# A four-layer graph network kernel: first rows in pairs of blocks, degree sums shared between VectorE and GpSimd, norms by ScalarE, and a new place for a block's own pair

## The chip, the cores and the metric

The kernel runs on one core of one Trainium2 chip. A core has five engines that run side by side, each with its own in-order queue: TensorE (PE, matrix products; its weight loads are listed as PEld), VectorE (DVE), ScalarE (ACT), GpSimd (POOL), and SyncE (SP), which here only starts DMA transfers. Matrix products go into PSUM, a small memory of banks; everything else lies in SBUF, which has 128 partitions. The metric is the device time of one execution in microseconds (us); lower is better. A measurement of this kernel can tell a change of about 2% from none.

## The reference

Four graph layers are applied to `x` (4096 rows of 64) with one dense matrix `adj` (4096 x 4096, float32, mostly zero). Each layer normalises the rows, applies a relu and adds its result to `x`:

```
h = relu(layernorm(x)); x = x + L0(h): relu((adj @ h) @ W.T + b)
h = relu(layernorm(x)); x = x + L1(h): q, k, h' = three "lorentz" linears of h
      att = adj * sigmoid((2 + 2 qm @ k.T) / att_scale + att_bias)
      s = att @ h';  s / sqrt(|inner(s)|)
h = relu(layernorm(x)); x = x + L2(h): w = adj / adj.sum(axis=1)          # the degree sums
      agg_i = sum_j w_ij logmap(h_i, h_j); v = agg @ weight + bias
      tanh(|v|) * v / |v|                                                 # the norms
h = relu(layernorm(x)); x = x + L3(h): rank-weighted sum over the last 100 neighbours
```

Layer 2 needs the degree of each row, that is the sum of its row of `adj`. Layers 0 and 1 read the same matrix, so the sums are collected while those layers run. Layer 2's distance between rows i and j is the same both ways, so a pair of blocks (i, j) is worked out once and used for both.

## The kernel before

**Tiles.** `adj` is read from HBM in transfers of 512 KB, each a *group*: two chunks of 128 source rows by 512 target rows, one SBUF tile of 128 x 1024 floats. The 4096 target rows make eight *blocks* (`ib`) of 512, and each block has 16 groups (`g`). The transposed matrix is read, so a group is the moving operand of a product and the sum builds up in a PSUM accumulator `acc`, one per block.

**Layers 0 and 1.** `l0_sums` multiplies each group of `adj` with the normalised rows `HA`. `before0` makes those rows, block by block: a sum over each row, the centred rows, ScalarE's squares, a second sum, a power by GpSimd (`power`, tile `ln_r`), and the product that writes `HA`. After each block, `after0` and `before1` turn its sums into the rows and the q and k of layer 1, with three more powers by GpSimd (`ln_r`, `lo_s` twice). Layer 1 makes, per group, the attention products (`l1_atts`, tile `mm`), ScalarE's sigmoid (`sig`), VectorE's product with `adj`, and the sum on TensorE. The last 12 groups of layer 0 are loaded in alternation with the first 12 of layer 1. Ten SBUF tiles hold groups of `adj` in these layers; a tile is loaded again when all of its readers are done.

**Degree sums.** `degree_sums` adds groups of `adj` into a tile `dg`, one full add of 128 x 1024 on VectorE for each group. The names in `LEFT` say which groups of a block wait until layer 1: four of 16 in blocks 1 to 6. A fold of `dg` and four products with a column of ones (`ones_f`) then give the degrees, in `after0` and, for blocks 1 to 6, again in `after1`.

**Layer 2.** `work` lists the items: for block i the columns J = i, i+1, ..., 7, each in two halves. An item with J > i is a *two*: its tile is also transposed and used for the other direction, through two banks of PSUM (`tr`), and the sums gather in `others`. The two items of the block's own pair (J = i) are shorter: the first (here marked `first`) is whole but its transposes are half as many, the second (`cut`) has half the targets. Per item there are, in order: products on TensorE (`mm`), a square on ScalarE, a clamp on GpSimd (`v<-v`), a logarithm and two exponentials on ScalarE, a VectorE step (`t<-mm,t`), a logarithm, a VectorE step (`t<-t,v`), the weights (`w<-t,adj`, `w<-tr,adj`), and the sums. Functions named `l2_...` hold these steps, and `in_steps` sets their order across neighbouring items. At the end of a block, `after2` turns the sums into rows, through both banks, with a power of eight columns by GpSimd (`r_nn`) for the two roots of the norm; `before3` follows with one more power (`ln_r`).

**Layer 3** is a stage of bf16 products behind layer 2, with masks from `adj` on VectorE.

**Order.** Every engine runs its instructions in the order in which the program issues them. That order is found when the kernel is built: `in_turn` takes, from all the generators (`feed`, `l0_sums`, `degree_sums`, `constants`, the `l2_...` stages and the row chains held in `tail`), the step that can start first by the planner's own costs (`Pace`). The chip then keeps that order even where an instruction waits. Two row chains can be under way at once, and each has one set of small tiles.

Of the kernel before, what the change touches and what calls it, by code (L numbers as in the profile page):

```python
# [18 lines left out]
P = 128  # L19
# [8 lines left out]
LEFT = (3, 7, 11, 15)  # L28
# [30 lines left out]
class Pace:  # L59
# [16 lines left out]
    def cost(self, engine, op, out, ins, rest, kw):  # L76
        n = per_partition(out)
        if engine == "PE":

            w, x = ins[0], ins[1]  # L80
            shape = [32 if k <= 32 else 64 if k <= 64 else 128 for k in (w.shape[0], per_partition(w))]
            change = 0.0 if shape == self.shape else 0.11
            self.shape = shape
            if op == "transpose":
                return change + 0.14
            share = 1 if n < 128 else min(128 * 128 // math.prod(shape), 4)
            passes = 4 if x.dtype == F32 else 1
            return change + max(passes * n / 2400 + 0.06, 0.27 if passes == 4 else 0.06) / share
        if engine == "ACT":
            if any(arg is AF.Sigmoid for arg in rest):  # L90
                n += n // 6
            return 0.18 + n / 1200 + (0.19 if "accum_out" in kw else 0.0)
        if engine == "POOL":
            return 1.65 if ALU.pow in kw.values() or n <= 8 else 0.25 + n / 300
        many = [ap for ap in ins if per_partition(ap) > 1]
        big = max([n] + [per_partition(ap) for ap in ins])
        psum = any(self.name(ap).split("_")[0] in ("mm", "acc", "tr") for ap in ins)
        return 0.12 + big / (1920 if len(many) <= 1 and not psum and op != "tensor_reduce" else 960)
# [38 lines left out]
def kernel(ctx: ExitStack, tc: tile.TileContext, a: dict, out: bass.AP):  # L137
# [93 lines left out]
    halves["both"] = const.tile([P, 2 * CB, 1], F32, name="halves")  # L231
    POOL.memset(halves["both"][:, 0:CB, :], 0.5)
    POOL.memset(halves["both"][:, CB :, :], -0.5)
# [15 lines left out]
    def later_constants():  # L249


        ACT.activation(es, scal[:, 0:3], AF.Exp)

        DVE.reciprocal(att_a, scal[:, 4:5])
        DVE.tensor_scalar(att_a, att_a, 2.0, None, ALU.mult)
        DVE.tensor_add(att_b, att_a, scal[:, 3:4])
        for t, one in [(t, 1.0) for t in rbs] + [(t, 0.25) for t in lbs]:
            POOL.memset(t, 0.0)
            for k in (1, 3):
                POOL.memset(t[:, :, k, 1:2], one)  # L260


        near_f = st["rows"].tile([P, P], F32, name="near_f", bufs=1)
        make_lower_triangular(nc, near_f, val=-STEP, diag=False)
        for q in range(4):
            b = slice(q * Q, (q + 1) * Q)
            DVE.tensor_copy(far[b, :], near_f[b, b])
        diag_f = st["rows"].tile([P, P], F32, name="diag_f", bufs=1)
        DVE.tensor_scalar(diag_f, ident, STEP * MAX_NEIGH, None, ALU.mult)
        DVE.tensor_add(near_f, near_f, diag_f)  # L270
        DVE.tensor_copy(near, near_f)


        DVE.memset(pick, 0.0)
        DVE.memset(spread, 0.0)
        for k in range(KH):
            DVE.memset(pick[:, k, k : k + 1], 1.0)
        for r in range(4):
            b = slice(r * Q, (r + 1) * Q)
            for h in range(2):  # L280
                to = spread[b, h, :, h * NC // 2 : (h + 1) * NC // 2]
                DVE.tensor_copy(
                    to.rearrange("p q (k r) -> p q k r", r=4)[:, :, :, r],
                    ident[b, r * Q : r * Q + KH].unsqueeze(1).to_broadcast([Q, 4, KH]),
                )
# [136 lines left out]
    def before0(ib, st):  # L422
        yield from layernorm_relu(ib, st["h0"][:, cs(ib), :])
# [124 lines left out]
    def after0(ib, acc, st):  # L548
        e = rows.tile([P, W], F32, tag="e", name="e")
        ACT.copy(e, acc)  # L550
        st["acc_free"][ib % 2] = pace.latest
        yield ON_V, lambda: st["dg_done"].get((0, ib))
        dg = st["dg"][0, ib]
        DVE.tensor_add(dg[:, 0, :], dg[:, 0, :], dg[:, 1, :])
        yield TURN

        ps = bank()
        v, n = ps[:, 0 : CB * D].rearrange("p (c k) -> p c k", k=D), CB * D
        for c in range(CB):
            b = slice(c * P, (c + 1) * P)  # L560
            PE.matmul(v[:, c, :], e[:, b], W0T, start=True, stop=True)
            PE.matmul(ps[:, n + c : n + c + 1], dg[:, 0, b], ones_f, start=True, stop=True)
        st["dg_free"][ib % 2] = pace.latest
        yield ON_V
        DVE.tensor_copy(deg[:, cs(ib), :], ps[:, n : n + CB].unsqueeze(2))
        s = rt("h", [P, CB, D])
        DVE.tensor_add(s, v, b0.to_broadcast([P, CB, D]))
        DVE.scalar_tensor_tensor(
            x[:, cs(ib), :], s, 0.0, x[:, cs(ib), :], ALU.max, ALU.add
        )  # L570
        yield ON_V

    def after1(ib, acc, st):
# [3 lines left out]
        yield ON_V, lambda: st["dg_done"].get((1, ib)) if (1, ib) in st["dg"] else 0.0  # L577
        dg = st["dg"].get((1, ib))
        if dg is not None:
            DVE.tensor_add(dg[:, 0, :], dg[:, 0, :], dg[:, 1, :])  # L580
        yield TURN
        ps = bank()
        v, n = ps[:, 0 : CB * D].rearrange("p (c k) -> p c k", k=D), CB * D
        for c in range(CB):
            b = slice(c * P, (c + 1) * P)
            PE.matmul(v[:, c, :], e[:, b], twice, start=True, stop=True)
            if dg is not None:
                PE.matmul(ps[:, n + c : n + c + 1], dg[:, 0, b], ones_f, start=True, stop=True)
        if dg is not None:
            st["dg_free"][ib % 2] = pace.latest  # L590
# [5 lines left out]
        if dg is not None:  # L596
            new = rt("r_c", [P, CB, 1])
            ACT.copy(new, ps[:, n : n + CB].unsqueeze(2))
        yield ON_V
        if dg is not None:  # L600
            DVE.tensor_add(deg[:, cs(ib), :], deg[:, cs(ib), :], new)
# [13 lines left out]
    def after2(ib, acc, others, st):  # L615
# [35 lines left out]
        n = rt("r_nn", [P, 2 * CB, 1])  # L651
        DVE.tensor_reduce(n[:, 0:CB, :], hz, AX.X, ALU.add)
        DVE.tensor_scalar(n[:, 0:CB, :], n[:, 0:CB, :], MIN_NORM * MIN_NORM, None, ALU.max)
        DVE.tensor_copy(n[:, CB :, :], n[:, 0:CB, :])

        POOL.tensor_tensor(n, n, halves["both"], ALU.pow)
        yield ON_S

        th = rt("r_c", [P, CB, 1])
        ACT.activation(th, n[:, 0:CB, :], AF.Exp, scale=-2.0)  # L660
# [3 lines left out]
        DVE.tensor_scalar(th, th, 2.0, -1.0, ALU.mult, ALU.add)  # L664
        DVE.tensor_mul(th, th, n[:, CB :, :])
        DVE.tensor_mul(tr, tr, th.to_broadcast([P, CB, D]))
# [47 lines left out]
    def in_turn(threads):  # L714
# [34 lines left out]
        "dg": {}, "dg_done": {}, "acc_free": [0.0, 0.0], "dg_free": [0.0, 0.0],  # L749
# [70 lines left out]
    def group(layer, ib, g):  # L820
        degree = (g in LEFT and 0 < ib < NB - 1) == (layer == 1)
        return {"layer": layer, "ib": ib, "g": g, "degree": degree, "left": 1 + degree, "at": 0.0}
# [31 lines left out]
    def degree_sums(layer, work):  # L854

        dg = st["dg"]
        for d in work:
            if not d["degree"]:
                continue
            first = (layer, d["ib"]) not in dg  # L860
            yield "DVE", lambda: latest(
                arrival(d, 3.0), st["dg_free"][d["ib"] % 2] if first else 0.0
            )
            if first:
                t = w01.tile([P, G, W], F32, tag="dg", name="dg", bufs=2)
                dg[layer, d["ib"]] = t
                st["dg_free"][d["ib"] % 2] = None
                DVE.tensor_copy(t, d["adj"])
            else:
                t = dg[layer, d["ib"]]  # L870
                DVE.tensor_add(t, t, d["adj"])
            used(d)
            if d is [e for e in work if e["degree"] and e["ib"] == d["ib"]][-1]:
                st["dg_done"][layer, d["ib"]] = pace.latest

    for ib in range(NB):
        follow(with_mark(0, ib, before0(ib, st)))
        tail[-1]["at"] = 4.5 + 0.4 * ib
# [13 lines left out]
    def constants():  # L892
# [5 lines left out]
        later_constants()  # L898
        loads.pop(0)

# [34 lines left out]
    def l1_sums():  # L935
        for pair in pairs:
# [23 lines left out]

    work = [
        {"ib": i, "J": j, "half": s, "g": j * (CB // G) + s, "first": i == j and s == 0,
         "last": j == NB - 1 and s == CB // G - 1, "two": i < j, "cut": i == j and s == 1,
         "left": 1 + (i == j and s == 1), "at": 0.0}
        for i in range(NB) for j in range(i, NB) for s in range(CB // G)
    ]
    twos = [d for d in work if d["two"]]
# [16 lines left out]
    def second_part():  # L984

        yield "ANY", lambda: latest(l1[-1].get("summed"), *st["dg_free"])
# [118 lines left out]
    def l2_turns():  # L1105
        for d in work:
# [6 lines left out]
            if d["first"]:  # L1113
# [24 lines left out]
    def l2_weights2():  # L1138
        k = -1
        for n, d in enumerate(work):  # L1140
            if d["first"]:
# [262 lines left out]
    def l3_sum():  # L1404
# [22 lines left out]
        if d["last"]:  # L1427
# [16 lines left out]
            (l2_coshs(), 0, once), (l2_weights2(), 1, lambda d: 2 if d["two"] else 1 if d["first"] else 0),  # L1444
        ),
        l2_clamps(), l2_gathers(), l3_weights(), l3_pass(), l3_counts(), l3_masks(),
        degree_sums(0, l0), degree_sums(1, l1), constants(),
# [46 lines left out]
```

## Time and profile before

Three runs took 1185.45, 1186.83 and 1261.08 us; the median is 1186.83.

| | |
|---|---|
| profiled execution, its own time | 1186.61 us |
| its span in the trace | 1184.6 us |
| PE / DVE / ACT / POOL busy | 1078.5 / 929.3 / 783.1 / 324.3 us |
| mean granted TensorE clock | 0.976 |
| read from HBM | 269.68 MB, mean 229 GB/s |
| DVE: degree adds of 128x1024 (`dg<-dg,adj`) | 114, 139.2 us |
| PE: products with the column of ones | 112 records, 18.8 us |
| POOL: clamps of 128x1024 | 64, mean 2925 ns |
| POOL: `r_nn` powers of 128x8 | 8, mean 2256 ns |

The span has four stages, which can be told by the tiles that the products read: layer 0 (`acc<-adj,HA`) from 16.7 to 211 us, layer 1 (`acc<-sig,HL`) from 194 to 485 us, layer 2 (`acc<-w,HA`) from 494 to 956 us, and layer 3 (`acc<-wt,S`) from 961 us on. A busy engine need not be the one that bounds its stage, and the means over the span mix stages with different bounds.

How to read the lines below: a row of the windows gives a stretch in us, its length, then the busy time of PE, PEld, DVE, ACT and POOL (with the number of instructions), the granted TensorE clock, the mean busy share of the DMA engines and GB/s. A row of the timeline gives start, length, engine, line of code, operation, tiles (out<-in), shapes, the count of merged instructions, and in brackets the idle time ahead of it with what ended it. Nearly all instructions are issued through one helper, so they share line 129 and are told apart by their tiles.

### The profile page before, as it was taken

The numbers are of one execution on the slowest core, as the hardware profiler recorded it, in microseconds if no ns is written. First come the engines' busy times: TensorE is split into PE (matmuls) and PEld (weight loads), VectorE is DVE, ScalarE is ACT, GpSimd is POOL, SyncE is SP. The second block draws the span as 40 slices with busy tenths as digits, with TensorE's granted clock in tenths as the row PEclk, the third lists the DMA queues.
The fourth block names the chain that finished last, engine by engine and source line by source line (L and its number), as shares of the span: only waits on it lengthen the run. The fifth ranks groups of instructions, "written<-read, shape, count | busy, mean of one in ns | idle before, by whom it ended". The sixth has DMA issues, their size and how long they took to land.

```text
span 1184.6 us, 15638 instructions
## 1 busy us (share of the span) xinstructions
PE 1078.5 (91%) x5367; PEld 449.7 (38%) x5392; DVE 929.3 (78%) x1523; ACT 783.1 (66%) x1250; POOL 324.3 (27%) x172
## 2 busy tenths in 40 slices
PE   3899999999999999889989989999889789999997
PEld 1234444333333333244444444444344333333332
DVE  6888888869988988688888888898989985555550
ACT  1055456777767766789988778787876655555554
POOL 2222321102000010344454464464654420000000
PEclk9898999999999999899999999999998999999999
DMA  7899999865777765535434534444364389888830
GB/s 275 330 405 350 401 378 348 303 216 199 245 249 235 249 232 192 195 107 196 162 128 172 175 121 166 160 150 163 113 206 151 124 343 367 321 314 312 303 112 9
DMA packets 77191, 271.76 MB, mean 229 GB/s; under 512 B 10040, under 2 KB 11064, under 8 KB 77112
## 3 DMA queue, kind: packets, MB, share of 16 engines
q1 hardware_dynamic: 75456, 270.57, 63.7%
q8 instruction: 42, 0.69, 0.2%
q10 hardware_dynamic: 1656, 0.20, 0.1%
q14 instruction: 37, 0.30, 0.1%
HBM read 269.68 MB, written 1.05 MB: 229 GB/s over the span
## 4 chain that ended last, share of the span: by engine, by line
PE 49%; DVE 18%; ACT 11%; issue 10%; POOL 8%; DMA 3%; SPq 0%; ACTq 0%; POOLq 0%; DVEq 0%
PE acc L129 23%; PE mm L129 17%; PE tr L129 8%; DVE dg L129 5%; POOL v L129 4%; ACT wt L129 3%; DVE w L129 3%; ACT v L129 2%; DMA adj<-in_adjT_dram 2%; ACT t L129 2%; DVE t L129 2%; POOL lo_s L129 1%; DVE sig L129 1%; ACT sig L129 1%; POOL ln_r L129 1%
## 5 line engine op out<-in xcount | busy, mean ns | idle before, releaser
L129 PE MATMUL acc<-w,HA 128*65 128x256 f32 (+1 forms) x736 | 256.3, 485 | 13.0 <-DVE others L129 7.1
L129 POOL TENSOR_SCALAR v<-v 128x1024 f32<-128x1024 f32 x72 | 204.8, 2845 | 211.5 <-ACT v L129 205.4
L129 ACT ACTIVATE wt<-mm 128x1024 uint16<-128x1024 f32 x124 | 120.3, 1021 | 94.1 <-PE mm L129 94.1
L129 ACT ACTIVATE sig<-mm,att_b,att_a 128x1024 f32<-128x1024 f32 x128 | 148.3, 1202 | 40.9 <-PE mm L129 39.9
L129 DVE TENSOR_TENSOR sig<-sig,adj 128x1024 f32<-128x1024 f32 x128 | 152.5, 1221 | 25.2 <-ACT sig L129 25.0
L129 PE MATMUL acc<-adj,HA 128*64 128x512 f32 x512 | 128.4, 639 | 24.3 <-DVE HA L129 24.1
L129 DVE TENSOR_TENSOR dg<-dg,adj 128x1024 f32<-128x1024 f32 x114 | 139.2, 1221 | 2.2 <-DMA adj<-in_adjT_dram 0.6
L129 PEld LDWEIGHTS acc<-w,HA 128*65 128x65 f32 x736 | 98.1, 143 | 104.7 <-issue 56.6
L129 PE MATMUL mm<-qT,kT 64*128 64x512 f32 x512 | 129.5, 619 | 3.3 <-ACT sig L129 3.3
L129 PE MATMUL acc<-sig,HL 128*64 128x512 f32 x512 | 123.3, 604 | 1.6 <-DVE sig L129 1.5
L129 DVE SCALAR_TENSOR_TENSOR t<-mm,t 128x1024 f32<-128x1024 f32 x72 | 83.6, 1161 | 44.4 <-ACT t L129 43.9
L129 PE MATMUL acc<-wt,S 128*64 128x512 bf16 (+1 forms) x479 | 97.7, 387 | 3.5 <-issue 2.4
L129 PE MATMUL mm<-RT,LT 64*128 64x512 f32 (+1 forms) x288 | 79.7, 631 | 15.9 <-DVE t L129 15.2
L129 ACT ACTIVATE t<-t 128x1024 f32<-128x1024 f32 x72 | 72.6, 1008 | 31.9 <-DVE t L129 31.3
L129 ACT ACTIVATE v<-mm 128x1024 f32<-128x1024 f32 x72 | 69.8, 970 | 30.7 <-PE mm L129 30.6
L129 POOL TENSOR_TENSOR ln_r<-ln_v,minus_half 128x4 f32<-128x4 f32 x32 | 49.3, 1542 | 148.7 <-DVE ln_v L129 148.7
L129 DVE TENSOR_TENSOR w<-t,adj 128x1024 f32<-128x1024 f32 x72 | 84.0, 1167 | 1.5
L129 DVE SCALAR_TENSOR_TENSOR t<-t,v 128x1024 f32<-128x1024 f32 x72 | 83.7, 1163 | 1.8 <-ACT t L129 0.9
L129 ACT ACTIVATE v<-v,minus 128x1024 f32<-128x1024 f32 x72 | 78.4, 1089 | 7.8 <-POOL v L129 7.7
L129 DVE TENSOR_TENSOR w<-tr,adj 128x512 f32<-128x512 f32 x120 | 77.5, 681 | 1.1 <-PE tr L129 1.1
L129 PE MATMUL tr<-ident,t 128*128 128x128 f32 x480 | 66.1, 280 | 11.9 <-DVE t L129 8.2
L129 DVE TENSOR_SCALAR RT<-adj 128x1024 bf16<-128x1024 f32 x74 | 50.4, 698 | 33.3 <-PE mm L129 33.0
(208 smaller groups left out, 1395.6 us busy)
## 6 DMA issues: line engine op xcount, KB each, us to landing
adj<-in_adjT_dram SPq DMA_DIRECT2D x512, 512.0 KB, 4.8
x<-in_x_dram SPq DMA_DIRECT2D x4, 256.0 KB, 3.7
out_dram<-h SPq DMA_DIRECT2D x8, 128.0 KB, 2.8
b<-in_b_dram ACTq DMA_DIRECT2D x2, 32.0 KB
W<-in_W_dram ACTq DMA_DIRECT2D x3, 16.0 KB, 4.4
W0T<-in_W0T_dram ACTq DMA_DIRECT2D x2, 16.0 KB, 3.4
W1T<-in_W1T_dram ACTq DMA_DIRECT2D x1, 16.0 KB, 3.4
W1T<-in_b_dram ACTq DMA_DIRECT2D x1, 0.2 KB
```

The costliest lines, as they stand in the source:

```text
L129: done = self.tc.keep_in_program_order(getattr(self.engine, op)(*args, **kw))
```

## The change

1. **First rows.** `before0` works on two blocks at a time: four chains of 128 x 512 elements in place of eight of 128 x 256. Their scratch space lies in tiles that layer 1 uses later (`HL`, `qT`) and in `lo_g`, `lo_t`, `lo_n`. The constants of layers 2 and 3, which were made at 36 us of the planner's time, are handed out as late steps (60 and 150 us).
2. **Degree sums.** Of a block's 16 groups VectorE adds eight, in layer 0 (`dg`); GpSimd adds four in layer 0 and four in layer 1, each as two adds of 128 x 512 straight into the block's part of `RT` (a tile that layer 2 fills later; the first group of a block needs one add). VectorE folds `dg` into `RT` with two adds. The products with the column of ones are gone from `after0`, and stand in `after1` for all eight blocks.
3. **Norms of layer 2's rows.** `after2` has no power by GpSimd any more: ScalarE takes a logarithm, two exponentials for the roots, and the exponential for the tanh. VectorE's part is two instructions shorter.
4. **Order of layer 2.** The columns of block i are now i+1, i, i+2, ..., so the own pair comes third and fourth. The first item of a block (`first`) and the start of an own pair (`own`) are told apart.
5. The planner's costs for GpSimd are changed, and `second_part` does not wait for `dg` any more.

```
-LEFT = (3, 7, 11, 15)
+POOL_0, POOL_1 = (3, 7, 11, 15,), (1, 5, 9, 13,)
+FRONT_0, FRONT_1 = (3, 7, 11, 15,), (1, 5, 9, 13,)
+ITSELF = 1
...
-            return 1.65 if ALU.pow in kw.values() or n <= 8 else 0.25 + n / 300
+            if op == "memset":
+                return 0.11 + n / 1200
+            return 0.5 + 0.25 * n if ALU.pow in rest else 0.25 + n / 390
...
-    def before0(ib, st):
-        yield from layernorm_relu(ib, st["h0"][:, cs(ib), :])
+    def before0(k, st):
+        c = slice(2 * k * CB, 2 * (k + 1) * CB)
+        xs, xc, to = x[:, c, :], st["HL"][:, c, :], st["h0"][:, c, :]
+        sq = st["qT"][:, 2 * k * W : (2 * k + 1) * W].rearrange("p (c d) -> p c d", d=D)
+        m, v, r = (rt(name, [P, 2 * CB, 1]) for name in ("lo_g", "lo_t", "lo_n"))
+        DVE.tensor_reduce(m, xs, AX.X, ALU.add)
+        DVE.scalar_tensor_tensor(xc, m.to_broadcast(xs.shape), -1.0 / D, xs, ALU.mult, ALU.add)
+        yield ON_S
+        ACT.activation(sq, xc, AF.Square)
+        yield ON_V
+        DVE.tensor_reduce(v, sq, AX.X, ALU.add)
+        DVE.tensor_scalar(v, v, 1.0 / D, LN_EPS, ALU.mult, ALU.add)
+        power(r, v, -0.5)
+        yield ON_V
+        DVE.scalar_tensor_tensor(to, xc, 0.0, r.to_broadcast(xs.shape), ALU.max, ALU.mult)
+        rows_at[0, 2 * k] = rows_at[0, 2 * k + 1] = pace.latest
...
-        n = rt("r_nn", [P, 2 * CB, 1])
-        DVE.tensor_reduce(n[:, 0:CB, :], hz, AX.X, ALU.add)
-        DVE.tensor_scalar(n[:, 0:CB, :], n[:, 0:CB, :], MIN_NORM * MIN_NORM, None, ALU.max)
-        DVE.tensor_copy(n[:, CB :, :], n[:, 0:CB, :])
-        POOL.tensor_tensor(n, n, halves["both"], ALU.pow)
+        n, one, th = (rt(name, [P, CB, 1]) for name in ("r_n", "r_m", "r_c"))
+        DVE.tensor_reduce(n, hz, AX.X, ALU.add)
+        DVE.tensor_scalar(n, n, MIN_NORM * MIN_NORM, None, ALU.max)
         yield ON_S
-        th = rt("r_c", [P, CB, 1])
-        ACT.activation(th, n[:, 0:CB, :], AF.Exp, scale=-2.0)
+        ACT.activation(n, n, AF.Ln)
+        ACT.activation(th, n, AF.Exp, scale=0.5)
+        ACT.activation(one, n, AF.Exp, scale=-0.5)
+        ACT.activation(th, th, AF.Exp, scale=-2.0)
         yield ON_V
...
     def group(layer, ib, g):
-        degree = (g in LEFT and 0 < ib < NB - 1) == (layer == 1)
+        late = g in (POOL_1 if ib else FRONT_1)
+        by = "POOL" if late or g in (POOL_0 if ib else FRONT_0) else "DVE"
+        degree = by if late == (layer == 1) else None
...
+            yield "DVE", lambda: opened.get(("sums", ib))
+            for c in range(G):
+                DVE.tensor_add(RT[:, ws(ib)], RT[:, ws(ib)], t[:, c, :])
...
+    def degree_sums_beside(work):
         for d in work:
+            if d["degree"] != "POOL":
+                continue
+            to, ib = RT[:, ws(d["ib"])], d["ib"]
+            yield "POOL", lambda: arrival(d, 3.0)
+            if ("sums", ib) in opened:
+                POOL.tensor_tensor(to, to, d["adj"][:, 0, :], ALU.add)
+                yield "POOL", lambda: 0.0
+                POOL.tensor_tensor(to, to, d["adj"][:, 1, :], ALU.add)
             else:
+                POOL.tensor_tensor(to, d["adj"][:, 0, :], d["adj"][:, 1, :], ALU.add)
+                opened["sums", ib] = pace.latest
...
+    def columns_of(i):
+        js = list(range(i + 1, NB))
+        return js[:ITSELF] + [i] + js[ITSELF:]
```

## The prediction

> **What bounds the kernel now.** I read the stages first (windows), then what PE waits for in each (timeline), then the ends of the blocks. The profiled execution took 1186.61 us for a span of 1184.6; the median of the three runs is 1186.83, so the sum below is made against 1186.6.
>
> ```profile
> 15.00:20.00 5.00, 3.30 (x8) 1.01 (x10) 4.85 (x11) 0.42 (x1) 0.42 (x1) 1.00 0.85 322
> 20.00:25.00 5.00, 4.70 (x20) 1.31 (x18) 4.90 (x12) 0.83 (x2) 1.59 (x2) 1.00 0.74 227
> 25.00:30.00 5.00, 3.40 (x16) 0.77 (x12) 3.01 (x8) 0.42 (x1) 1.06 (x2) 1.00 0.48 143
> ...
> 100.00:150.00 50.00, 47.22 (x258) 21.56 (x256) 41.45 (x68) 24.27 (x99) 14.36 (x7) 1.00 0.99 382
> ...
> 300.00:350.00 50.00, 49.62 (x230) 18.37 (x228) 45.00 (x86) 36.09 (x69) 2.85 (x2) 1.00 0.76 251
> ```
>
> Layer 0 (100 to 150) is bound by the loads: DMA busy 0.99, 382 GB/s, with PE close behind. Its start is not: DMA falls to 143 GB/s, because PE has no rows and the ten tiles stay full. Layer 1 (300 to 350) is bound by PE, 49.6 of 50.
>
> ```profile
> 16.22 0.42 DVE L129 SCALAR_TENSOR_TENSOR HA<-ln_xc,ln_r 128x256 f32<-128x256 f32 x1
> ...
> 41.68 0.43 DVE L129 SCALAR_TENSOR_TENSOR HA<-ln_xc,ln_r 128x256 f32<-128x256 f32 x1
> ...
> 42.16 10.18 PE L129 MATMUL acc<-adj,HA 128*64 128x512 f32 x40 [3.42 <-DVE HA L129]
> ```
>
> The first rows come at 16.2 and the last at 42.1 us, with degree adds and constants on VectorE between them. Then the end of a block in layer 2:
>
> ```profile
> 693.35 1.09 PE L129 MATMUL tr<-ident,t 128*128 128x128 f32 x8 [1.29 <-DVE t L129]
> ...
> 698.65 1.13 PE L129 MATMUL mm<-RT,LT 64*128 64x512 f32 x4 [2.11 <-DVE t L129]
> ...
> 700.63 3.46 PE L129 MATMUL acc<-w,HA 128*65 128x256 f32 x8 [0.53 <-DVE w L129]
> ```
>
> ```profile
> 692.10 2.72 POOL L129 TENSOR_TENSOR r_nn<-r_nn,halves 128x8 f32<-128x8 f32 x1 [0.91 <-DVE r_nn L129]
> ```
>
> In steady state PE is full: a two takes 5.85 us, and two of them 12.25 with a wait of 0.5 for `others`. At a block's end PE waits three times (1.29, 2.11, 0.53), and the eight products behind the gap take 3.46 us where they take 1.94 elsewhere, at a granted clock of 0.79 (698 to 702). `e<-acc,others` comes at 679.4, 755.5, 819.3 and 870.9: the gaps 76.1, 63.8 and 51.6 fall by 12.25, so 14.8 us per block remain for its own pair and the rows. PE's own work in that is 8.4 (first item 3.6, cut 2.75, rows 2.0); some 6.4 us per block are lost.
>
> **The change part by part.**
>
> *First rows: -12.* A chain of 512 elements costs VectorE three instructions of 0.69 (rows of 128x512) and one of 0.17, so four chains take 9 us where eight take 15 (1.87 each). ScalarE's square is 0.59 (a 128x512 square), the power of eight columns 2.06 (`lo_s`). From x at 4.4, the first HA ends near 11 and, with the one copy and one add of `dg` between, the last near 20-21. PE then has rows whenever a group is there, and DMA need not fall. Against some 400 GB/s (the windows around reach 409 to 419), 15 to 50 us lack 78+173+257+175+4+85+114 GB/s over 5 us each: 4.4 MB, 11 us. I take 12, as the half clock of 32 to 38 us should go too. Bounds: 4 (only PE's first 6 us, partly) and 16 (first `e` at 45.5 instead of some 30). The constants that go to later steps cost VectorE 4 us in layer 0, beside the loads.
>
> *Products with ones, early attention: -2.* Sixteen records with ones and without (52.3 to 54.2) take 1.9 us, so a block's ones cost 0.95. Eight blocks lose them in layer 0 (7.6 us, mostly behind DMA); layer 1 goes from six to eight, +1.9. In the built order three pairs of attention products (1.92 each) run in layer 0 before its last block, where the old order had them near its end: -5.8 from PE's stage, of which I let a third count, as the row chain of block 7 (33 us, from 212 to 245) holds groups 14 and 15 and would be late next. Bounds -6 and +4.
>
> *Degree sums: +4.* VectorE loses per block of layer 0 11 adds of 1.22 and a copy (14.8 with the fold) and gets 10.6; in layer 1 it loses 5.0. GpSimd gets 120 adds, which no row shows. Nearest:
>
> ```profile
> L129 POOL TENSOR_TENSOR x<-x,b x8: 721/727/1076, 617.8 to 977.2; 128x256 f32<-128x256 f32 x8
> ...
> L129 DVE SCALAR_TENSOR_TENSOR hb<-ln_xc,ln_r x8: 468/1256/1267, 615.1 to 977.6; 128x256 f32<-128x256 f32 x8
> ```
>
> Twice the half-size add is 1.45 us (2.15 by the slowest). Seven in layer 0 and the powers of a chain (1.54+1.74+2.06) fill 15.5 of 21.4 us per block. Three powers per chain can wait behind an add, 1.45 each; behind them wait the chain's VectorE product and its transposes, in a chain of some 45 us with two under way. The second row is the dangerous one: this step takes 0.42 in layer 0 but 1.26 when it starts beside a clamp of GpSimd, +0.84. Both engines then read SBUF. At 0.84 per add, VectorE per layer 1 block has 30 - 5.0 + 8 x 0.84 = 31.7 of 34 us, and in layer 0 17.8 - 14.8 + 10.6 + 7 x 0.84 = 19.5 of 21.4: both fit, with stalls. At 1.45, 36.6 and 23.8: over by 2.6 and 2.4, that is 21 and 17 us in all. So 0 to +38; I take +4, by the 0.84 row.
>
> [...]
>
> *Norms: in the next sum.* Gone are a power of 2.72 us, a copy of 0.17 and one more small VectorE step; ScalarE gets three more of 0.20. The chain is 2.3 us shorter, and the clamp behind the power (0.8 late at 694.8) is not held. What is late next is ScalarE.
>
> *Own pair behind the first pair, with the norms: -18.* The row chain now lies beside the first pair of twos, where PE has 11.7 + 2.0 us of work, and the own pair's light steps come later. ScalarE's load over both pairs is 2 x 5.33 (squares 1.02, logarithms 1.14 and 1.06, exponentials 1.05 and 1.06) + 8.5 (own pair, the cut at half shape) + 3.4 (rows, with the new steps) = 22.5, and 1.2 for the 0.2 us that it waits for VectorE in each item: 23.7. PE needs 20.7. So 23.7 - 12.25 = 11.5 remain per block where 14.8 do now: -3.3 for five blocks and half of that for the sixth. Bounds: PE's 8.4 in six blocks, -38; on the other side the row chain now needs a `tr` bank three times while each two needs both, held for 0.36 to 1.0 us (the ScalarE copies and VectorE reads), +2.5 per block, +15. I take ScalarE's load, as it is the row that binds after the stall. At the start of layer 2 the second-direction tiles are wanted two items sooner; their loads are issued at 485.7, ahead of everything but six groups, and hidden by 490-495's row chain.
>
> *Last block: -2.* It has only its own pair; there the shorter norm counts directly.
>
> Layer 3 stays. Sum: 1186.6 - 12 - 2 + 4 - 18 - 2 = 1156.6, forecast **1157**.
>
> **The rivals.**
>
> *Slower: the shared reads bind VectorE.* Place: layer 1, where every product `sig<-sig,adj` reads SBUF twice. VectorE has 25 us of 34 without adds, so it becomes the bound from 1.1 us of lost time per GpSimd add. At 1.45: +38, and the start's gain is eaten in layer 0: 1186.6 - 20 + 38 = 1205. At 2.15 layer 1 needs 42 us per block and layer 0 28.7: +115, 1280. For it: the 1.26 row; the clamps of layer 2 run mostly beside VectorE steps that read PSUM. Against: 0.84 is under 1.1.
>
> *The first two layers give nothing.* Powers behind adds delay the chains as much as the rows come sooner; layer 2 alone gains: 1186.6 - 20 = 1167.
>
> *The own pair moves without effect.* Banks or ScalarE keep the 14.8; then 1186.6 - 12 - 2 + 4 - 2 = 1175.
>
> *Better.* PE's floor in layer 2 and 15 from the start: 1186.6 - 15 - 2 + 2 - 38 = 1134.
>
> **How the numbers follow.** Forecast (1147 to 1164) 0.52, no gain in the first layers 0.18, own pair without effect 0.12, better 0.08, slower 0.10. A change of 2% is 1163. Faster: 0.48 + 0.08 + 0.04 of the second case = 0.60. Slower by 2% (above 1210.6): 0.08. Same: 0.32. The range takes in half of the better case and both smaller gains, 1138 to 1182; it leaves the slower case out, and what lies under 1138.
>
> **What would show it.** First rows: HA complete by about 21 us, DMA above 350 GB/s from 15 us on, last layer 0 product near 199. Sums: GpSimd's adds near 1.45 us, `sig<-sig,adj` lengthened from its 1.22, PE still 97% busy in layer 1, which ends near 475. Layer 2: 76.1 becomes about 73 between the ends of the blocks, and no PE gap over 1.5 us behind the last sums. Wrong it would be if `sig<-sig,adj` averaged above 1.6 us, if PE waited for `HL` or `qT` in layer 0, or if the new gaps lay behind the cut item.

## The result and the profile after

The changed kernel took **1232.67 us** (median of four runs, 1225.62 to 1235.18), against 1186.14 for the kernel before beside it: a ratio of 1.0388, 95% interval 1.0363 to 1.0413. It is slower by 46 us; the forecast was 1157, and the result lies outside the range, on the side of the slower rival.

The copies that end the blocks' sums (the starts of `e<-acc` and `e<-acc,others`) cut the span into four parts:

| us | layer 0 until its last sum | layer 1 | to layer 2's first sum | from there to the end | span |
|---|---|---|---|---|---|
| before | 211.6 | 274.0 | 105.9 | 593.1 | 1184.6 |
| after | 238.8 | 297.4 | 105.6 | 589.2 | 1231.0 |
| difference | **+27.2** | **+23.4** | -0.3 | -3.9 | +46.4 |

So the whole loss is in the two layers that collect the degree sums, and layers 2 and 3 together gave 4 us of the 20 that were forecast for layer 2. The windows of the kernel after, with the columns of those shown of before:

```profile
15.00:20.00 5.00, 5.00 (x23) 1.52 (x20) 4.45 (x8) 0.63 (x1) 3.91 (x3) 1.00 1.03 409
20.00:25.00 5.00, 4.23 (x20) 0.82 (x16) 4.96 (x3) 0.00 (x0) 4.76 (x4) 1.00 0.66 230
25.00:30.00 5.00, 2.66 (x12) 0.42 (x8) 4.93 (x3) 0.00 (x0) 3.92 (x2) 0.97 0.51 173
...
100.00:150.00 50.00, 44.54 (x202) 18.01 (x204) 42.43 (x50) 23.44 (x89) 29.26 (x19) 0.90 0.86 311
...
300.00:350.00 50.00, 44.31 (x206) 16.62 (x204) 43.70 (x94) 32.49 (x71) 21.47 (x15) 1.00 0.60 199
```

The start is as forecast until 20 us (PE full, 409 GB/s), and then the loads fall again. From 100 to 150 the DMA share is 0.86 where it was 0.99, and in layer 1 PE is busy for 44.3 of 50 us where it was 49.6. VectorE has 42.4 and 43.7 of 50 in these rows: it is not full in either.

What PE waits for in layer 0 (the table of waits; sum in us, number, longest), first before (45 to 212 us), then after (45 to 239 us):

```profile
PE tr L129 <- DVE HL L129: 3.8, 6, 1.2
PE tr L129 <- DVE h L129: 2.5, 2, 1.6
PE tr L129 <- ACT qq L129: 1.1, 2, 0.6
```

```profile
PE tr L134 <- DVE HL L134: 14.6, 7, 4.1
PE tr L134 <- DVE h L134: 7.4, 6, 2.1
PE tr L134 <- ACT qq L134: 5.7, 4, 1.9
```

PE stands at the transposes of the row chains, 28 us instead of 7. In all, PE is idle for 29.1 us between 45 us and the last sum, where it was for 7.7: 21 of the 27 us. The other 6 are longer busy time, at a mean granted clock of 0.94 instead of 0.98. In layer 1 PE's busy time did not grow (267.5 us before, 266.9 after); all 23 us there are idle time.

The VectorE steps that PE waits for have become longer, which the summaries by tile show (shortest, median and longest in ns, first and last start), before and after:

```profile
L129 DVE TENSOR_TENSOR sig<-sig,adj x128: 1217/1220/1227, 187.7 to 481.5; 128x1024 f32<-128x1024 f32 x128
L129 DVE TENSOR_TENSOR HL<-hb,lo_s x8: 412/420/422, 72.4 to 236.9; 128x252 f32<-128x252 f32 x8
```

```profile
L134 DVE TENSOR_TENSOR sig<-sig,adj x128: 1210/1224/2304, 203.6 to 527.6; 128x1024 f32<-128x1024 f32 x128
L134 DVE TENSOR_TENSOR HL<-hb,lo_s x8: 1477/1478/1490, 56.6 to 264.4; 128x252 f32<-128x252 f32 x8
L134 POOL TENSOR_TENSOR RT<-RT,adj x112: 1257/1652/2557, 20.8 to 505.8; 128x512 f32<-128x512 f32 x112
```

More than half of the sigmoid products keep their 1.22 us, the longest take 2.30 (the mean is 1491 ns). GpSimd's own add takes 1.27 when left alone (at 35.38), and up to 2.56: **both** engines lose. And the step `HL<-hb,lo_s` loses 1.06 us all eight times. Why every time in this kernel, the timeline of after shows, one collision in layer 0 (VectorE, GpSimd, PE) and one in layer 1:

```profile
171.11 1.48 DVE L134 TENSOR_TENSOR HL<-hb,lo_s 128x252 f32<-128x252 f32 x1 [1.13 <-POOL lo_s L134]
...
171.04 2.67 POOL L134 TENSOR_TENSOR RT<-RT,adj 128x512 f32<-128x512 f32 x2
...
172.73 0.60 PE L134 MATMUL tr<-ident,HL 128*64 128x128 f32 x4 [1.24 <-DVE HL L134]
...
354.79 3.43 DVE L134 TENSOR_TENSOR sig<-sig,adj 128x1024 f32<-128x1024 f32 x2
...
353.06 4.08 POOL L134 TENSOR_TENSOR RT<-RT,adj 128x512 f32<-128x512 f32 x2 [2.31 <-DMA adj<-in_adjT_dram]
```

`HL` waits for a power by GpSimd. When the power ends, GpSimd goes straight on with the next add in its queue, and VectorE's step starts 0.07 us later beside it. The end of the power thus starts both, here GpSimd's first. In layer 1, two products take 3.43 in place of 2.44 beside two adds that take 4.08 in place of 2.61 (at 64.42, where VectorE is idle).

The boundary of the first two blocks of layer 2 in the timeline of after:

```profile
732.43 0.63 PE L134 MATMUL tr<-ident,t 128*128 128x128 f32 x4 [1.57 <-DVE l L134]
...
751.36 1.93 PE L134 MATMUL acc<-w,HA 128*65 128x512 f32 x4 [1.81 <-DVE w L134]
754.66 1.13 PE L134 MATMUL mm<-RT,LT 64*128 64x512 f32 x4 [1.37 <-DVE t L134]
...
757.01 1.97 PE L134 MATMUL tr<-ident,t 128*128 128x128 f32 x8 [0.89 <-DVE t L134]
758.77 2.58 PE L134 MATMUL acc<-w,HA 128*65 128x512 f32 x4
```

The stall behind the last sums has gone, and the same time stands elsewhere: PE waits for a bank of the row chain at 732, and behind the cut item at 751 to 757, where the products then run longer again (2.58 for 1.88).

### The profile page after: what moved, and what is told of

It reads as the page before. It is cut to its first block, busy times and chain, and to the rows that moved or that the text cites. A ratio compares the mean times of both kernels' runs of the same rounds, so it can differ in the third digit from the quotient of the medians.

```text
span 1231.0 us, 15536 instructions
## 1 busy us (share of the span) xinstructions
PE 1087.4 (88%) x5318; PEld 442.9 (36%) x5344; DVE 950.0 (77%) x1411; ACT 788.9 (64%) x1272; POOL 494.4 (40%) x278
## 4 chain that ended last, share of the span: by engine, by line
PE 39%; DVE 24%; issue 13%; ACT 11%; POOL 8%; DMA 4%; ACTq 0%; POOLq 0%; SPq 0%; DVEq 0%
PE acc L134 19%; PE mm L134 13%; PE tr L134 6%; DVE sig L134 4%; DVE w L134 4%; DMA adj<-in_adjT_dram 3%; ACT wt L134 3%; DVE t L134 3%; POOL RT L134 3%; ACT v L134 2%; DVE dg L134 2%; POOL lo_s L134 2%; ACT t L134 2%; ACT sig L134 2%; DVE r_n L134 1%
## 5 line engine op out<-in xcount | busy, mean ns | idle before, releaser
L134 POOL TENSOR_SCALAR v<-v 128x1024 f32<-128x1024 f32 x72 | 201.0, 2791 | 260.8 <-ACT v L134 230.6
L134 POOL TENSOR_TENSOR RT<-RT,adj 128x512 f32<-128x512 f32 x112 | 189.2, 1691 | 128.7 <-DMA adj<-in_adjT_dram 106.9
L134 DVE TENSOR_TENSOR sig<-sig,adj 128x1024 f32<-128x1024 f32 x128 | 187.1, 1491 | 28.7 <-ACT sig L134 27.7
L134 PE MATMUL acc<-adj,HA 128*64 128x512 f32 x512 | 135.0, 655 | 17.8 <-DVE HA L134 11.0
L134 PE MATMUL mm<-qT,kT 64*128 64x512 f32 x512 | 132.5, 631 | 15.8 <-ACT sig L134 15.4
L134 PEld LDWEIGHTS acc<-w,HA 128*65 128x65 f32 x736 | 95.9, 140 | 110.7 <-issue 50.4
L134 PE MATMUL acc<-sig,HL 128*64 128x512 f32 x512 | 127.2, 613 | 8.2 <-DVE sig L134 7.5
L134 DVE TENSOR_TENSOR dg<-dg,adj 128x1024 f32<-128x1024 f32 x56 | 85.5, 1526 | 1.4 <-DMA adj<-in_adjT_dram 0.7
L134 PE MATMUL tr<-ident,t 128*128 128x128 f32 x480 | 69.4, 285 | 16.3 <-DVE l L134 8.1
L134 ACT ACTIVATE t<-t 128x1024 f32<-128x1024 f32 x72 | 72.6, 1008 | 17.5 <-DVE t L134 17.5
L134 PEld LDWEIGHTS mm<-qT,kT 64*128 64x128 f32 x512 | 43.8, 189 | 88.3 <-ACT sig L134 45.9
```

Source lines behind the costliest of these rows:

```text
L134: done = self.tc.keep_in_program_order(getattr(self.engine, op)(*args, **kw))
```

## The experiments

Three theories were to be told apart for the degree sums: GpSimd's adds lengthen VectorE's products because both read operands from SBUF ("shared reads"); the adds stand in the way in GpSimd's in-order queue; or the new order of the program is at fault. The parts of the table for all the kernels (us; the medians are compared with runs of the kernel before on the same chip, 1185.41 or 1186.01):

| | layer 0 | layer 1 | to first sum | to the end | median | ratio, 95% interval |
|---|---|---|---|---|---|---|
| e2 sums alone | 236.3 | 294.2 | 111.1 | 591.6 | 1236.43 | 1.0432 (1.0409 to 1.0456) |
| e6 writes for adds | 210.8 | 273.9 | 111.2 | 591.9 | 1189.23 | 1.0024 (1.0009 to 1.0038) |
| e9 one operand | 211.2 | 277.0 | 111.2 | 591.9 | 1194.64 | 1.0073 (1.0056 to 1.0090) |
| e10 adds in layer 1 only | 212.1 | 294.1 | 110.9 | 591.9 | 1210.10 | 1.0203 (1.0186 to 1.0219) |
| e7 adds in layer 0 only | 248.8 | 275.4 | 112.9 | 590.0 | 1230.14 | 1.0378 (1.0363 to 1.0393) |
| e1 all but the sums | 206.6 | 293.1 | 105.3 | 586.8 | 1193.59 | 1.0062 (1.0042 to 1.0082) |
| e12 planner costs alone | 216.5 | 278.6 | 100.7 | 590.6 | 1188.75 | 1.0024 (1.0007 to 1.0042) |
| e11 all but sums, old costs | 208.1 | 275.8 | 108.5 | 587.9 | **1182.37** | **0.9964** (0.9951 to 0.9977) |
| e5 first rows alone | 207.5 | 279.9 | 104.4 | 591.8 | 1185.70 | 1.0009 (0.9992 to 1.0026) |
| e3 norms alone | 211.4 | 275.6 | 105.6 | 591.3 | 1185.46 | 0.9998 (0.9984 to 1.0012) |
| e4 own pair alone | 210.3 | 277.5 | 108.4 | 598.9 | 1195.23 | 1.0066 (1.0040 to 1.0092) |
| e8 norms and own pair | 210.7 | 277.5 | 108.6 | 589.4 | 1184.90 | 1.0000 (0.9989 to 1.0011) |

**e2: the degree sums alone**, with the planner's new costs.

```
 the kernel before, with
-        degree_sums(0, l0), degree_sums(1, l1),
+        degree_sums(), degree_sums_beside(l0), degree_sums_beside(l1),
```

> The kernel before with the new degree sums (and the planner's costs for them), nothing else. 'Shared reads': all of the loss and more, since the gains of the rest are missing: 1235 to 1250, sig<-sig,adj near 1.49 us, GpSimd's adds 1.26 to 2.5 us. 'Order': at most half of the loss, 1186 to 1210.

1236.43: the sums alone cost more than the whole change, and all but 5 us of it in the same two layers. The rest of the change then takes some 4 off (1236.43 to 1232.67, not measured beside each other). `HL` collides five times of eight here. Where it starts 0.06 us behind an add (at 61.58) it takes 1.48 us and the add 1.26; where it starts 0.16 ahead of one (at 92.04) it takes 0.41 and the add 1.38. In these rows the one that starts first keeps its length.

**e6: writes in place of the adds.** As e2, but GpSimd writes where it added; its eight groups of a block are not summed. The planner's cost of such a write is set to 0.65, about half of an add's.

```
-                POOL.tensor_tensor(to, to, d["adj"][:, 0, :], ALU.add)
...
+                POOL.memset(to, 0.0)
+                POOL.memset(to, 0.0)
+                POOL.tensor_tensor(to[:, 0:8], to[:, 0:8], d["adj"][:, c, 0:8], ALU.add)
```

> The new degree sums alone, but each add of 128x512 on GpSimd is two memsets of 128x512 to the same tile (which read nothing) and an add of eight columns, which keeps the wait for the group and its release; GpSimd's degree sums are thereby left out. Theory A (VectorE and GpSimd hold each other up while both read two operands): sig<-sig,adj back near 1.22 us, no rows of 1.0 us and more for HL, and 1185 to 1200 in all. Theory B (it is GpSimd's in-order queue: powers of the row chains stand behind the adds, and groups come free late): about as with the adds, 1220 or more.

1189.23. GpSimd is about as busy as in e2 (498.6 and 516.6 us), the powers stand behind nearly as much work, the groups are held nearly as long: two writes of 0.53 us and an add of 0.48 are 1.54 us against 1.69. Yet layers 0 and 1 are back at 210.8 and 273.9, and the summaries by tile are those of before:

```profile
L132 DVE TENSOR_TENSOR sig<-sig,adj x128: 1210/1224/1273, 178.9 to 476.5; 128x1024 f32<-128x1024 f32 x128
L132 DVE TENSOR_TENSOR HL<-hb,lo_s x8: 414/420/423, 57.8 to 231.5; 128x252 f32<-128x252 f32 x8
```

The result is the one of theory A, and the queue does not explain the loss. Nor does the order: in the traces of e2, e6 and e9 (below) VectorE's 1447 and ScalarE's 1252 instructions stand in the same order, and so do PE's, but for 25 records that are missing in e2 and e6. Of e2's 51 us the 47 over e6 go with the adds in place of the writes; 4 stay in e6, whose way to layer 2's first sum is 5 us longer too (111.2 for 105.9).

The run shows a second thing: VectorE has 58 adds fewer than before (56 for 114 of 1.22 us) and GpSimd harms nobody, and still nothing is won. **The adds that the change takes off VectorE had cost no time that shows** (e12 below, with the new costs and all the old adds, takes 1188.75).

**e9: one operand in place of two.** As e6, with a GpSimd instruction that reads one operand.

```
-                POOL.tensor_tensor(to, to, d["adj"][:, 0, :], ALU.add)
+                POOL.tensor_scalar(to, d["adj"][:, 0, :], 0.0, None, ALU.max)
```

> The new degree sums alone, but each add of 128x512 on GpSimd is a max with zero of the same group's 128x512 into the same tile: one operand read in place of two, about 1.4 us each by the clamp's 2.86 for 1024; GpSimd's degree sums are thereby left out. Theory A1 (it is the second operand that VectorE and GpSimd cannot both read): sig<-sig,adj back at 1.22 us, HL at 0.42, about 1187. Theory A2 (any reading by GpSimd holds VectorE's products up): sig<-sig,adj stays near 1.4 to 1.5, 1225 or more.

1194.64, near A1 but not on it. The tile summaries, `sig` and `HL` of VectorE and GpSimd's new instruction:

```profile
L132 DVE TENSOR_TENSOR sig<-sig,adj x128: 1211/1225/1652, 178.4 to 479.9; 128x1024 f32<-128x1024 f32 x128
L132 DVE TENSOR_TENSOR HL<-hb,lo_s x8: 414/828/834, 58.3 to 232.0; 128x252 f32<-128x252 f32 x8
L132 POOL TENSOR_SCALAR RT<-adj x120: 1483/1524/2724, 16.2 to 460.1; 128x512 f32<-128x512 f32 x120
```

A one-operand instruction of 1.48 us adds 0.41 to a VectorE step beside it, where a two-operand one of 1.26 adds 1.06; at worst `sig` loses 0.43 instead of 1.08. The instructions that read one operand cost 5 us more than the writes, which read none; the adds, which read two, cost 47 more (e2 against e6). The instruction of e9 is also another kind (a maximum with a constant, not an addition), and so is the write of e6, so whether the count of operands or the kind makes these differences is not shown; that it is GpSimd's adds that cost the time, is.

**e10 and e7: GpSimd's adds in one layer only.** VectorE adds the other twelve groups of a block in layer 0. In e10 VectorE's fold opens `RT`, so that it does not wait for GpSimd.

```
e10: +POOL_0, POOL_1 = (), (1, 5, 9, 13,)
     +FRONT_0, FRONT_1 = (), (1, 5, 9, 13,)
     +            DVE.tensor_add(RT[:, ws(ib)], t[:, 0, :], t[:, 1, :])
e7:  +POOL_0, POOL_1 = (3, 7, 11, 15,), ()
     +FRONT_0, FRONT_1 = (3, 7, 11, 15,), ()
```

> The new degree sums alone, with VectorE adding twelve groups of a block in layer 0 and GpSimd four in layer 1, none on GpSimd in layer 0. If GpSimd's adds cost where they run: layer 0 ends near 211 as before, layer 1 takes 290 to 297 us, and about 1205 to 1213 in all. If layer 1 was longer only because of its late and disordered start: layer 1 near 275 and about 1190.

> The new degree sums alone, with GpSimd adding four groups of a block in layer 0, VectorE the other twelve in layer 0, and none added in layer 1. Theory A (each GpSimd add in layer 1 costs what it does to the sigmoid products beside it): layer 1 falls from 294 to about 275 to 280 us and sig<-sig,adj in it returns to 1.22; layer 0 ends no sooner than at 236; about 1215 to 1225. Theory B (layer 1 is longer because of a worse order or a late start): layer 1 stays at 290 or more, and the time at 1235.

e10 took 1210.10: layer 0 ends at 212.1 as before, layer 1 takes 294.1. e7 is the mirror image: layer 1 takes 275.4, `sig` is at a mean of 1.23, and layer 0 ends at 248.8. The layer is right and the total is missed (1230.14, not 1215 to 1225), probably because VectorE takes twelve groups of a block there instead of eight, each add longer (mean 1.42), and is busy for 45 to 48 of 50 us in layer 0. So **the adds cost where they run**, and a late start or a new order is not needed to explain layer 1. PE's waits in layer 1 (275 to 480 us), of before, of e10 and of after:

```profile
PE mm L129 <- ACT sig L129: 1.8, 5, 0.4
```

```profile
PE mm L132 <- ACT sig L132: 9.7, 12, 2.1
```

```profile
PE mm L134 <- ACT sig L134: 13.0, 12, 2.3
```

Over the whole of layer 1 these waits are 3.3, 14.0 and 14.7 us, and PE's waits for VectorE's products themselves (`acc` behind `sig`) 1.5, 6.3 and 7.1. The bank that PE wants is read by ScalarE's sigmoid. Why the sigmoid is late, the timeline of after shows at its longest such wait:

```profile
389.77 2.67 POOL L134 TENSOR_TENSOR RT<-RT,adj 128x512 f32<-128x512 f32 x2 [1.36 <-DMA adj<-in_adjT_dram]
389.81 1.50 DVE L134 SCALAR_TENSOR_TENSOR ln_xc<-ln_m,x 128x256 f32<-128x256 f32 x1
391.41 0.42 ACT L134 ACTIVATE r_sq<-ln_xc 128x256 f32<-128x256 f32 x1 [1.95 <-DVE ln_xc L134]
391.73 2.28 ACT L134 ACTIVATE sig<-mm,att_b,att_a 128x1024 f32<-128x1024 f32 x2
392.97 1.13 PE L134 MATMUL mm<-qT,kT 64*128 64x512 f32 x4 [2.33 <-ACT sig L134]
```

A step of a row chain (`ln_xc`, 0.42 us elsewhere) starts beside GpSimd's adds and takes 1.50; ScalarE's square waits for it, the sigmoid stands behind the square in ScalarE's queue, and PE behind the sigmoid. In five of the waits of the kernel after, 8.9 of the 14.7 us, the sigmoid stands behind this square; in three of them, 6.6 us, `ln_xc` itself was lengthened (1.23 to 1.50).

**e1, e12 and e11: everything but the sums, and the planner's costs.** e1 is the change without part 2 (layer 2 again waits for `dg`); e12 is the kernel before with part 5's costs alone; e11 is parts 1, 3 and 4 with the old costs.

```
e1, e11: -        degree_sums(), degree_sums_beside(l0), degree_sums_beside(l1),
         +        degree_sums(0, l0), degree_sums(1, l1),
e12, e1: +            return 0.5 + 0.25 * n if ALU.pow in rest else 0.25 + n / 390
```

> The changed kernel with the degree sums of the kernel before (VectorE alone, tile dg). Theory 'shared reads': VectorE steps that read SBUF twice and GpSimd's adds shut each other out, and this cost all of the loss in layers 0 and 1 (50 us). Then sig<-sig,adj is back at 1.22 us and HL<-hb,lo_s at 0.42, layer 0's last sum is copied near 200 to 204, layer 1 lasts 274 us, and the time is 1164 to 1174. Rival 'order': the first rows, the early attention products or the late constants spoiled the order of layers 0 and 1; then the time stays at 1200 or above with the steps at their old lengths.

> The kernel before with only the planner's new costs for GpSimd. Theory A (the costs by themselves move layer 1's start): 1190 to 1196, with the loss between 200 and 260 us. Theory B (they only matter with GpSimd's adds): 1185, stages as before.

> First rows, norms and own pair with the old degree sums, and with the planner's old costs (the run with the new costs took 1193.6, layer 1 in it 293 us). Theory A (the new costs put layer 1's start in a bad order): layer 1 near 275 to 280 and 1180 to 1186. Theory B (the early first rows and the old sums do not go together): layer 1 stays near 290 and 1193.

e1 was a surprise: without the sums, layer 1 still took 293.1. e12 shows that the planner's costs alone do a quarter of that (278.6), and e11 that without them layer 1 takes 275.8. So it comes with the pairing of the new costs with the rest. In e1's layer 1 PE is busy for 277.9 us with 1222 records, where before has 267.5 with as many, at a granted clock of 0.96 instead of 1.00, and idle for 8.7 us more; what sets off the lower clock is open. That this is a part of the changed kernel's 46 us isn't seen: e2 has the whole loss without the rest of the change, and PE's busy time in layer 1 is as before in the kernel after. **e11 beats both kernels**, by 0.36% (interval 0.23% to 0.49%) against before; as the order alone moves more than that (e12), no part of the change can be credited with it.

**e5: first rows alone.**

```
-        follow(with_mark(0, ib, before0(ib, st)))
+        follow(before0(k, st))
...
+    degree_sums(0, l0), degree_sums(1, l1), constants(), *later_constants(),
```

> The kernel before with the first rows in pairs and the late constants, nothing else; the planner's costs are the old ones. Theory A (the prediction's step): the first block of layer 0 ends some 8 us sooner and the gain stays, so about 1174. Theory B (layer 0 is set by its row chains and its loads, so an early start does not reach its end): the first block ends some 8 us sooner, the last block of layer 0 at most 5 us sooner, and layer 1 gives part of it back: 1182 to 1195.

As theory B says. The first sum ends at 39.8 instead of 45.5, the last at 207.5 instead of 211.6, and layer 1 gives back 5.9. The windows of e5 show where; they are the only stretches of its layer 1 between 300 and 480 us whose granted clock is below 0.97, and before has none there:

```profile
310.00:315.00 5.00, 5.00 (x17) 1.64 (x17) 2.98 (x8) 3.12 (x5) 1.01 (x1) 0.66 0.35 112
...
380.00:385.00 5.00, 5.00 (x22) 2.60 (x22) 2.61 (x8) 2.74 (x5) 1.01 (x1) 0.68 0.53 182
...
450.00:460.00 10.00, 9.68 (x44) 4.24 (x42) 6.30 (x14) 5.60 (x9) 1.01 (x1) 0.83 0.59 188
```

By an estimate from these clocks, each is worth some 1.7 us (5 x 0.34, 5 x 0.32, 10 x 0.17), 5 in all, at the ends of three blocks; a fourth like them lies at 242 to 246 us. What sets them off there is open: PE waits for 0.32 us at such a boundary in both kernels.

**e3, e4, e8: norms, own pair, and both.**

```
e3, e8: -        POOL.tensor_tensor(n, n, halves["both"], ALU.pow)
        +        ACT.activation(n, n, AF.Ln)
        +        ACT.activation(th, n, AF.Exp, scale=0.5)
        +        ACT.activation(one, n, AF.Exp, scale=-0.5)
e4, e8: +        return js[:ITSELF] + [i] + js[ITSELF:]
```

> The kernel before with the norms by ScalarE in layer 2's rows. Theory 'chain': the stall behind a block's end hangs on the row chain (2.3 us shorter now), so the gaps between the ends of the blocks fall by 1 to 2.5 us each from 76.1, 63.8 and 51.6, and the time is 1170 to 1180. Rival 'short items': PE runs dry because the own pair's items are short and ScalarE's chain of an item is long; then the gaps stay within 0.5 us and the time is 1182 to 1188.

> The kernel before with the own pair behind the first other pair. 'Short items': the stall moves with the own pair, behind its cut item, and the gaps between the ends of the blocks stay or grow by 1 to 2 us, as the row chain (with its long power) now takes PSUM banks from the twos; time 1184 to 1195. The forecast's view (ScalarE's load alone remains): gaps 2 to 3 us smaller, time 1168 to 1176.

> The kernel before with the norms by ScalarE and the own pair behind the first other pair, with the old degree sums and first rows. Theory A (the two parts only pay together: the norms shorten the chain that the moved own pair has to hide): layer 2 takes some 461 us in place of 471, layer 3 gives 3 back, about 1180. Theory B (each part as alone): 1195, as the own pair alone. The prediction's own step would give 1168.

In e3 the three gaps are 75.1, 62.9 and 50.4 us, about 1 shorter each, as 'chain' has it, and the time is that of 'short items'. In e4 they are 75.3, 64.1 and 52.7, in e8 74.3, 62.1 and 50.4.

From layer 2's first sum to the end the kernel before takes 593.1 us; the norms alone 591.3, the own pair alone 598.9, both 589.4. The two parts do work together (-3.7 where the sum of them alone is +4.0), but the forecast's 18 to 20 us are not there, and 2.7 go again in the first block (108.6 for 105.9) and 3.5 in layer 1. The trace of e4 is of the slowest of its six runs (1188.25 to 1196.83 us), that of e8 3 us above its median, so these parts are rough. That e8 brought 1184.90 and not 1180 is a miss of theory A in size.

A part of the gain in layer 2 is given back behind it, in e3 3.5 of 5.2 us and in e8 5.6 of 9.1. In e11 the last sum of layer 2 ends at 945.5, 353.1 us after the first (365.1 before), and from there the end is 234.8 us away instead of 228.0. The windows of e11 behind that sum:

```profile
945.52:955.52 10.00, 7.12 (x33) 2.44 (x32) 8.86 (x25) 6.64 (x10) 1.89 (x2) 0.79 0.85 314
955.52:965.52 10.00, 10.00 (x56) 3.99 (x54) 7.98 (x19) 4.51 (x12) 0.00 (x0) 0.70 1.03 415
```

PE is busy for 216.9 us behind the last sum where it was 207.1 before. Some 5 of that are, by an estimate from these rows, the lower clock of these 20 us (10 x 0.21 + 10 x 0.30), and some 3 are layer 3's products that before had run in the gaps of layer 2's last blocks: PE spends 5.0 us on them before the last sum in the kernel before, 1.9 in e11.

## Why the prediction was wrong

**What bounds the kernel now.** The reading of layer 0 (loads, DMA 0.99) and layer 1 (PE, 49.6 of 50) was right: where loads and PE bind, VectorE's 114 adds stand beside other work. The forecast had no gain from moving them (+4), and e6, which takes 58 of them away without harm, wins nothing. So the sums could hardly have given more than zero.

**Degree sums: the step that failed**, forecast at +4 and measured at +51 by e2, outside its bounds of 0 to +38. What failed is the rule by which a collision was charged: it was to cost time only where VectorE's work no longer fits a block ("both fit, with stalls"; the bound "from 1.1 us of lost time per GpSimd add"). The +4 itself is not worked out from the 0.84 that it names.

- *The price of a collision* was about right as a mean, by luck. The +0.84 came from a step beside a clamp, which reads one operand. Beside a two-operand add, `HL` lost 1.06 of the add's 1.26, while more than half of the sigmoid products lost nothing. In e10 `sig` rose from 1.221 to 1.487 us over 128 products, 34 us, and the other VectorE steps of layer 1 took some 16 more; over 64 adds that is 0.8 us.
- *The threshold* failed. With 0.8 per add VectorE is busy for 30.8 us of each block in e10's layer 1, near the 31.7 that the prediction worked out and found to fit into 34. The block still took 36.8 instead of 34.3: the layer is 20.1 us longer, 0.31 us per add. A step that comes late is enough where ScalarE and PE stand behind it in their queues; VectorE need not be full.
- *The order of events.* "Three powers per chain can wait behind an add" looked at the queue ahead of the power. What happened is behind it: the end of a power releases VectorE's step and GpSimd's next add together, so that `HL` collided eight times of eight in the changed kernel (five of eight in e2). With two chains under way and their transposes among PE's products, PE waited 28 us for them in place of 7, and the loads fell to a DMA share of 0.86.

The slower rival named the mechanism, with VectorE full in layer 1 as its condition and 1205 as its price at 1.45 per add. The condition was not met, over half of the loss was in layer 0, and its price was 28 us too low (1205 against 1232.67). Among the marks that were to show the forecast wrong, PE waiting for `HL` in layer 0 and gaps behind the cut item came true; `sig` at a mean above 1.6 did not (1.49), as the loss needed less.

**First rows: -12** was 4 at the end of layer 0 and nothing in the total (e5, 1.0009). The rows came as worked out: the last `HA` of after ends at 21.2 us, as "20-21" said. The failed term is the 4.4 MB of missed loads: with the rows early, the loads fall all the same (e5: 146 GB/s from 25 to 30 us, where before had 143). VectorE is full in e5 from 15 to 35 us (4.66 to 4.93 of each 5), and a group that it still has to add keeps its tile; that this is what holds the loads was not tested by itself. The half clock that was to go as well stayed: from 30 to 45 us the granted clock is 0.66 in e5 as in before. The lower bound, 4, was the right value at the end of layer 0, and layer 1 took 5.9 back, most of it in spells of a lower clock.

**Products with ones, early attention: -2.** Not tested by itself. In e6, which has the products with ones where the change has them, layer 0 ends 0.8 sooner and layer 1 takes the same.

**Norms and own pair: -18 and -2** was -3.9 in the changed kernel from layer 2's first sum to the end. The norm chain works as described (three more ScalarE steps of 0.20 us in place of a power of 2.26 on average). From its first to its last sum layer 2 is 7.4 us shorter (365.1 to 357.7), but not where it was forecast: the gaps between the ends of the blocks are 77.0, 63.6 and 52.3 instead of 76.1, 63.8 and 51.6, with about 73 forecast for the first, and PE is idle for 39.1 us in it where it was for 37.6. What got shorter lies mostly at its ends: the first of these gaps (85.6 for 87.9, ahead of the three) and the last (11.4 for 17.5, forecast at -2).

The failed term is "ScalarE's load, as it is the row that binds after the stall": the waits at 732 to 757 (1.57 + 1.81 + 1.37 + 0.89 = 5.6 us) are nearly the 6.4 that were to go; the first is for a bank of the row chain, and the other three stand behind the cut item, where PE waits for VectorE. The two pairs took 28.0 us (77.0 less four times 12.25) where 23.7 was forecast, and from 727.4 us on ScalarE is busy for 19.9 of these 28.0: it was not the row that bound them. For the own pair alone even the sign was that of the bound for banks (e4, +5.8 in the trace of its slowest run).

**Layer 3 stays** was off by 3.5 in the kernel after (231.5 for 228.0), and by 6.8 in e11, where some 3 us are layer 3's products that no longer run in the gaps of layer 2's last blocks: such gaps are not all lost time.

## What to carry to other kernels

Before work is moved from VectorE to GpSimd, ask whether it costs anything where it is, and test that by leaving it out. Where it is moved, measure what GpSimd's instruction does to the VectorE steps beside it: here writes left VectorE's two-operand products at 1.22 us, instructions that read one operand cost 5 us more in all (e9 against e6), and adds that read two cost 47 (e2 against e6). That the busy time of an engine still fits is no proof that a lengthened step is free: look at who stands behind it in the other queues. A chain that hands over from GpSimd to VectorE can meet GpSimd's next instruction at that very moment, as `HL` did here eight times of eight, so what comes next in that queue matters.

## What the runs showed that was not expected

- The loss goes both ways: GpSimd's add of 128x512 took 1.27 us alone and up to 2.56 beside VectorE's product of 1.22, and that product up to 2.30.
- VectorE's one-operand steps are not spared: the copy `dg<-adj` of 128x1024, 0.69 us before, took 1.75 two times of eight in the kernel after (at 172.51 beside the second of two adds), and its mean rose to 0.95.
- The planner's costs for GpSimd, which change only the order of the instructions, moved the stages by several us in both directions (e12: layers 0 and 1 +9.5, the rest -7.7), and came with 11 us beside the other parts (e1 against e11). A kernel whose order is planned from costs has this much play in every comparison of one edit.
